# Expert tiles of 256, 192 and 128 slots in one form, and a routing step rearranged beside the last SwiGLU

## The chip, the cores and the metric

The kernel runs on one core of one Trainium2 chip. The core has a matrix engine (TensorE, "PE" in the profile, its weight loads "PEld"), a vector engine (VectorE, DVE), an activation engine (ScalarE, ACT), a general engine (GpSimd, POOL) and a queue engine (SyncE, SP) that issues most transfers. The metric is the time of one execution in device microseconds; the kernel before takes 730.28 us, the median of three runs (728.83 to 730.33). All times below are microseconds unless marked ns.

## The reference

The input x has 8 sequences of 256 tokens with 256 features, 2048 tokens in all. Four layers follow, each with a residual sum; all arithmetic is fp32.

```
x = x + L0(x)   # conditioned RMS norm, attention of 16 heads, conditioned RMS norm, SwiGLU of width 1024
x = x + L1(x)   # attention with a key mask, RMS norm of its output, modulation by the condition
x = x + L2(x)   # a fixed 4x4 rotation per feature (quaternions, with a gate)
x = x + L3(x)   # mixture of experts:
    gate = xn @ wg_W + wg_b + (genre_embed @ gg_W + gg_b)
    topk_w, topk_i = top_k(softmax(gate), 2)
    h1 = relu(x @ W1[e] + b1[e]); h2 = relu(h1 @ W2[e] + b2[e]); y = h2 @ W3[e] + b3[e]
    out = sum over a token's two experts of weight * y
```

L3 has 8 experts (256 to 512 to 512 to 256). With two experts per token there are 4096 pairs of token and expert, called slots here. Evaluated on these inputs, the reference's routing gives the experts 173, 190, 600, 732, 754, 773, 450 and 424 slots.

## The kernel before, in words

The tokens go through L0, L1 and L2 by sequence (b = 0 to 7), as a pipeline. The list `queue` fixes the order of attention steps (`block`, four per sequence and layer), and `run` puts pieces of other work between them: projections, SwiGLU pieces, normalisations. TensorE's instructions run in the order of the text throughout; up to the last attention, VectorE's and ScalarE's do too (`text_order`), so an instruction that waits holds up everything written after it on its engine. Most matmul results pass through three rotating PSUM banks (`bank`, pool `ps_m`): a fourth result waits until the first has been read.

`swiglu(b)` (lines 1082 to 1095) makes eight pieces of products, pg and ph in turn, each of four fp32 matmuls. pg is turned into sg by ScalarE and VectorE, ph is multiplied with it into hT, and then come four pieces of the output product pd.

Two sequences make a group (g = 0 to 3, 512 tokens). `rotate` (lines 1156 to 1167) applies L2 and writes the group's rows to the DRAM tables `tokens` and `out`; `route` (1179 to 1237) finds each token's two experts; `place_choices` (1244 to 1261) counts places with the matmul pk, and POOL scatters a record of token number and weight into the DRAM list `slots`, where each expert has a region of its own.

`table` turns the experts' counts into a list of tiles: which expert, and where its records begin. It is a chain of tiny VectorE instructions on one partition. The first table is made when three of four groups are routed: five tiles of 256 slots are sure to be full by then, whatever the last group holds. The second, after the last group, gives the rest: 12 whole tiles and, with `half_table`, two places for half tiles, for experts whose rest is 128 slots or fewer. Tiles beyond that would run in a conditional part after the main one.

`experts` runs a list of tiles as a pipeline on TensorE. Per tile: `records` reads the slot records (SP), `fetch` the expert's weights (SP, 2180 KB, three buffers in turn), `gather` the tokens' rows (POOL), `flip` transposes them, `hidden` makes h1 and h2 (weights stationary, 256 slots as columns, lines 1461 to 1471), `give` makes y with the slots stationary and adds the rows into `out` by indirect DMA (1489 to 1509). Within tile n the order is h1 of n, y of n-1, flip of n+1, h2 of n. A half tile is made in another form by `half` (1524 to 1555): its 128 slots are stationary and 512 weight columns move past them; each hidden layer is then transposed back by four transposes. Its steps are laid between those of a whole tile.

At the start of the kernel, `conditioned` flips the first sequence into one bank, VectorE scales both halves of it (line 912), and a few dummy matmuls (`keep_busy`, tile pw) fill TensorE meanwhile. Near the end of the pipeline, the loop step i = 6 has `late_=(4,)`: the follow-up of block 4, `after_second(4)` with its copies o<-py (line 1129), is held back until block 5 has been issued.

## Time and profile before

| what | value |
|---|---|
| median of three runs | 730.28 |
| profiled execution | 731.9 |
| its span, first to last instruction | 729.7 |
| TensorE busy | 710.9 (97%) |
| VectorE, ScalarE, POOL busy | 366.0, 258.7, 183.1 |
| expert tiles begin, last matmul ends | 452, 720 |
| granted TensorE clock, mean | 0.988 |

A group of instructions is shown as line, engine, operation, result and operands by the program's names, shapes and count. A busy time of matmuls counts each pass from issue to result, and passes overlap, so what one costs is read from the distance between starts. A wait is printed as who waited, for which instruction, how long in total, how often, and the longest. In a stretch's row come the busy times of PE, PEld, DVE, ACT and POOL, each with its count, then the granted clock, the share of DMA time and GB/s. In a timeline a row has start, duration, engine, line, operation and operands, and in square brackets the idle time before it with what ended it.

### The profile page before, as it was taken

Reading aid. Unit: us, or ns where it says so; the run is one execution under the profiler, and the core shown is the slowest. Engines: PE = TensorE matmul, PEld = TensorE weight load, DVE = VectorE, ACT = ScalarE, POOL = GpSimd, SP = SyncE. Lnnn points to the kernel's source line nnn. Section 1 sums busy time; section 2 is a strip of 40 time slices with the busy share of each in tenths; the row PEclk is TensorE's granted clock in tenths of the full one; section 3 lists DMA queues with packets and bytes.
Section 4 is the critical chain, followed back from the end, with each engine's and each line's share of the span. In section 5 each row is a group of like instructions: output and inputs, shape, how many; then the busy total and the mean of one; then the engine's idle time right before and its main releaser. Section 6 shows DMA issues by size and latency. Waiting matters only on the chain.

```text
span 729.7 us, 11080 instructions
## 1 busy us (share of the span) xinstructions
PE 710.9 (97%) x4242; PEld 539.5 (74%) x4242; DVE 366.0 (50%) x1129; ACT 258.7 (35%) x414; POOL 183.1 (25%) x219
## 2 busy tenths in 40 slices
PE   8999999999999999999999989999999999999994
PEld 7567777667666766766677856788888788788883
DVE  5557444575586764586854754777122222222221
ACT  2653335444454444454542315332121222221220
POOL 4312601000001311000500044126452424433113
PEclk9999999999999999999999989999999999999997
DMA  9400000000010000010000225464784586676512
GB/s 300 149 16 16 0 1 15 12 4 16 15 60 14 16 1 1 15 58 1 17 1 1 73 90 177 178 195 139 220 258 152 166 275 188 203 241 236 158 15 33
DMA packets 27005, 68.03 MB, mean 93 GB/s; under 512 B 8312, under 2 KB 21120, under 8 KB 24512
## 3 DMA queue, kind: packets, MB, share of 16 engines
q1 hardware_dynamic: 17904, 55.21, 22.0%
q0 software_dynamic: 8752, 11.85, 7.5%
q8 instruction: 35, 0.57, 0.4%
q14 instruction: 26, 0.21, 0.1%
q10 hardware_dynamic: 288, 0.18, 0.1%
HBM read 57.44 MB, written 9.79 MB: 92 GB/s over the span
## 4 chain that ended last, share of the span: by engine, by line
PE 89%; DVE 6%; ACT 1%; issue 1%; DMA 0%; POOL 0%; POOLq 0%; DVEq 0%; ACTq 0%
PE ph_a L1461 17%; PE s_a L976 9%; PE pg L1082 8%; PE o_a L989 8%; PE pd L1095 8%; PE ph L1082 8%; PE pe_a L1489 5%; PE ph_s L1461 5%; PE pq_a L920 4%; PE pk_a L920 4%; PE py L1012 2%; PE pv_a L950 2%; PE py L1128 2%; PE pe_s L1489 2%; PE pv_a L942 2%; PE ph_a_h L1534 1%
## 5 line engine op out<-in xcount | busy, mean ns | idle before, releaser
L978 ACT ACTIVATE pe_a<-s_a 128x2048 f32<-128x2048 f32 x64 | 120.1, 1877 | 116.9 <-PE s_a L976 116.7
L1461 PE MATMUL ph_a<-h_a,w_a 128*128 128x256 f32 x384 | 85.5, 379 | 0.0
L1461 PEld LDWEIGHTS ph_a<-h_a,w_a 128*128 128x128 f32 x384 | 72.1, 190 | 10.2 <-issue 1.0
L976 PE MATMUL s_a<-qz_a,kT_a 32*128 32x512 f32 x512 | 74.1, 647 | 0.7 <-ACT pe_a L978 0.2
L1471 DVE TENSOR_SCALAR h_a<-ph_a,w_a 128x256 f32<-128x256 f32 x48 | 23.2, 483 | 92.1 <-PE ph_a L1461 91.1
L1082 PE MATMUL pg<-xT_n,gate_wT 128*128 128x256 f32 x256 | 61.9, 385 | 0.0
L989 PE MATMUL o_a<-pe_a,va 128*32 128x256 f32 x1024 | 61.9, 382 | 0.0
L1082 PE MATMUL ph<-xT_n,hid_wT 128*128 128x256 f32 x256 | 61.5, 383 | 0.0
L1095 PE MATMUL pd<-out_wT,hT 128*128 128x256 f32 x256 | 61.1, 392 | 0.0
L989 PEld LDWEIGHTS o_a<-pe_a,va 128*32 128x32 f32 x1024 | 30.0, 109 | 39.9 <-issue 23.4
L1095 PEld LDWEIGHTS pd<-out_wT,hT 128*128 128x128 f32 x256 | 49.0, 195 | 13.6 <-issue 4.0
L1469 ACT ACTIVATE h_a<-ph_a,w_a 128x256 f32<-128x256 f32 x48 | 22.8, 475 | 97.8 <-DVE h_a L1471 97.8
L1082 PEld LDWEIGHTS ph<-xT_n,hid_wT 128*128 128x128 f32 x256 | 47.8, 190 | 13.0 <-DVE y L1054 3.0
L1082 PEld LDWEIGHTS pg<-xT_n,gate_wT 128*128 128x128 f32 x256 | 47.5, 190 | 12.7 <-issue 3.2
L1509 POOL DMA_INDIRECT out<-ye_a,trec_a x24 | 38.0, 1584 | 63.3 <-ACT ye_a L1507 53.4
L1055 POOL TENSOR_TENSOR xy<-y,x 128x512 f32<-128x512 f32 x8 | 10.2, 1271 | 142.1 <-DVE y L1054 87.2
L1461 PE MATMUL ph_a<-xt_a,w_a 128*128 128x256 f32 x192 | 43.7, 379 | 0.0
L998 DVE STREAM_TRANSPOSE tu_a<-o_a 128x512 f32<-128x512 f32 x32 | 22.8, 712 | 39.5 <-PE o_a L989 39.5
L1261 POOL DMA_INDIRECT slots<-rec,posi x32 | 31.8, 995 | 42.4 <-DVE r_mine L1251 32.9
L1489 PE MATMUL pe_a<-w_a,h_a 128*128 128x256 f32 x184 | 42.1, 379 | 0.0
L1461 PEld LDWEIGHTS ph_a<-xt_a,w_a 128*128 128x128 f32 x192 | 36.3, 190 | 4.9
L1489 PEld LDWEIGHTS pe_a<-w_a,h_a 128*128 128x128 f32 x184 | 34.7, 190 | 5.7 <-issue 1.0
(310 smaller groups left out, 1062.6 us busy)
## 6 DMA issues: line engine op xcount, KB each, us to landing
w_a<-in_experts SPq DMA_DIRECT2D x12, 2180.0 KB, 9.3
w_s<-in_experts SPq DMA_DIRECT2D x5, 2180.0 KB, 10.3
w_a_h<-in_experts SPq DMA_DIRECT2D x2, 2180.0 KB, 9.1
mod<-mod_rows SPq DMA_DIRECT2D x8, 256.0 KB, 3.3
tokens<-x SPq DMA_DIRECT2D x4, 512.0 KB, 3.2
out<-x SPq DMA_DIRECT2D x4, 512.0 KB, 4.2
x<-in_x SPq DMA_DIRECT2D x7, 256.0 KB, 2.8
gate_wT<-in_gate_wT SPq DMA_DIRECT2D x1, 1024.0 KB, 9.0
```

What stands on the lines that cost most here:

```text
L920: nc.tensor.matmul(pp[:, c, :], w[:, k, c * P : (c + 1) * P], xT[:, k, :], start=k == 0, stop=k == KC - 1)
L976: nc.tensor.matmul(sc[:, j], kT[r, c, kc * P : (kc + 1) * P], qz[r, c], start=True, stop=True)
L978: nc.scalar.activation(pe, sc, AF.Exp)
L989: nc.tensor.matmul(o[32 * i : 32 * i + 32, qd, :], va[:, kc, 8 * c + 4 * qd + i].rearrange("p a d -> p (a d)"), pe[:, 2 * qd + i // 2, i % ...
L998: nc.vector.transpose(turned.rearrange("p q j a d -> p (q j a d)"), o.rearrange("p q s -> p (q s)"))
L1082: nc.tensor.matmul(ps[:, j, :], w[:, k, o : o + P], yT[:, k, :], start=k == 0, stop=k == KC - 1)
L1095: nc.tensor.matmul(pd[:, t, :], hT[:, c, t * P : (t + 1) * P], out_w[:, c, :], start=c == 0, stop=c == HID // P - 1)
L1261: sc = nc.gpsimd.indirect_dma_start(out=slots, out_offset=bass.IndirectOffsetOnAxis(ap=posi[:, t : t + 1], axis=0), in_=rec[:, t, :], in_o ...
L1461: nc.tensor.matmul(ph[:, c - c0, :], w[:, o : o + P], src[:, k, :], start=k == 0, stop=k == n_in - 1)
L1471: nc.vector.tensor_scalar(h[:, c, :], ph[:, c - c0, :], bias, 0.0, ALU.add, ALU.max)
L1489: nc.tensor.matmul(pos[q][:, q, :], h2[:, k, q * P : (q + 1) * P], w[:, o : o + D], start=k == 0, stop=k == MC - 1,)
L1509: ad = nc.gpsimd.indirect_dma_start(out=out[0:reach, :], out_offset=bass.IndirectOffsetOnAxis(ap=rec[:, q, 0:1], axis=0), in_=y[:, q, :], ...
```

## The change

- Tiles have one form in three sizes: 256 slots (two column blocks of 128), 192 (two of 96) and 128 (one). All run weights-stationary through `hidden` and `give`, one after another in the order `ORDER`; `half` is gone. The rest is now 9 whole tiles, three of 192 and two of 128. `parts_table` lists both smaller kinds, by the count of full steps of 64 slots.
- One sure tile, the early one, is listed from the first two groups (`first_table`, now run in loop step 6 right after `place_choices(1)`); the other four by `second_table`, beside the first block of the last `run("bbb")`. The early tile's weights, record and rows are asked for when its pools open, before the last two sequences' work.
- In the last group of pieces before `place_choices(2)`, the steps of the rotation and routing of group 2 stand differently among the SwiGLU pieces: (0, 0, 1, 1, 2, 1, 2, 0) pieces ahead of the eight steps and two after them, instead of (0, 2, 1, 1, 2, 1, 1, 0) and one.
- The first sequence is flipped into two banks, and ScalarE scales the second half.
- Two memsets on POOL stand before four of its loads instead of after them.

```
-HALF = SL // 2
-NBIG = (2 * T + E * (HALF - 1)) // SL
-ALWAYS = 12
-HALVES = 2
-
-BESIDE = (3, 6)
+QUARTER = SL // 4
+SMALLER = ((2, 96), (1, 128))
+NBIG = (2 * T + E * (QUARTER - 1)) // SL
+ALWAYS = 9
+PARTS = (3, 2)
+
+ORDER = "ww1w0w1w0w0www"
...
     quats = small_in[:, 0 : B + 4 + 1]
+    for va in va_bufs["a0"]:
+        nc.gpsimd.memset(va, 1.0)
     wcT = load(nc.gpsimd, a["WcT"], [C, 2 * D], "WcT", pool=pool_b)
...
-    def conditioned(xs, b, j, name, eng=(nc.vector, nc.vector)):
-        pt = flipped(xs, name)
+    def conditioned(xs, b, j, name, eng=(nc.vector, nc.vector), apart=False):
+        if apart:
+
+            pts = [bank(f"pt_{name}_{k}", (P, S)) for k in range(KC)]
+            for k in range(KC):
+                for t in range(NQ):
+                    nc.tensor.transpose(pts[k][:, t * P : (t + 1) * P], xs[:, t, k * P : (k + 1) * P], ident)
...
+        nt = row(f"nt_{key}", [E])
+        nc.vector.tensor_tensor(nt, each[:, :, nh - 1], done[:, 0:E], ALU.subtract)
...
+        if op is ALU.is_ge:
+
+            now = row(f"now_{key}", [E])
+            nc.vector.tensor_tensor(now, end, nt, ALU.subtract)
+            nc.vector.tensor_scalar(now, now, -1.0, float(n_tiles), ALU.mult, ALU.add)
+            nc.vector.scalar_tensor_tensor(now, now, 0.0, nt, ALU.max, ALU.min)
+            nc.vector.tensor_tensor(done[:, 0:E], done[:, 0:E], now, ALU.add)
+        return end, each
+
+    def parts_table(each):
+
+        n = row("n_p", [2, E])
+        nc.vector.tensor_tensor(n[:, 0, :], each[:, :, 2], each[:, :, 3], ALU.subtract)
+        nc.vector.tensor_tensor(n[:, 1, :], each[:, :, 0], each[:, :, 2], ALU.subtract)
...
     def first_table():
-        nt, end, todos["sure"], _ = table("sure", (NG - 1) * NTG, SURE, ALU.is_ge)
...
+        table("early", (NG - 2) * NTG, EARLY, ALU.is_ge)
+        yield
+
+    def second_table():
+        table("sure", (NG - 1) * NTG, SURE - EARLY, ALU.is_ge)
         yield
...
+    def whole(key, n):
+
+        return f"{key}{n}", lambda what: todos[key][0:1, what, n : n + 1], NQ2, P
+
+    def smaller(size, n):
+        return f"p{size}_{n}", lambda what: todos["parts"][0:1, what, size, n : n + 1], *SMALLER[size]
+
+    def experts(items, pl, key, early=0, near_end=None):
...
         def hidden(n, src, n_in, off, boff, name):
-            w = st[n]["w"]
+            w, many = st[n]["w"], items[n][2] * items[n][3]
...
                         nc.tensor.matmul(
-                            ph[:, c - c0, :], w[:, o : o + P], src[:, k, :], start=k == 0, stop=k == n_in - 1
+                            ph[:, c - c0, 0:many], w[:, o : o + P], src[:, k, 0:many],
+                            start=k == 0, stop=k == n_in - 1,
                         )
...
-        placed = at_once(place_choices(i // 2 - 2)) if i in (4, 6) else once(compare_queries) if i == 2 else iter(())
+        placed = {
+            2: lambda: once(compare_queries), 4: lambda: at_once(place_choices(0)),
+            6: lambda: at_once(place_choices(1), first_table()),
+        }.get(i, lambda: iter(()))()
...
     pl = expert_pools(life_a, life_b2)
+    others_ = []
+    sure = experts(
+        [whole("early", n) for n in range(EARLY)] + [whole("sure", n) for n in range(SURE - EARLY)],
+        pl, "s", EARLY, near_end=(next(others_[0]) for _ in range(1)),
+    )
+    next(sure)
...
-    for n in (0, 2, 1, 1, 2, 1, 1, 0):
+    for n in (0, 0, 1, 1, 2, 1, 2, 0):
         for _ in range(n):
             next(pieces)
         next(rotated, None)
     do(rotated)
     next(pieces)
+    next(pieces)
     do(place_choices(NG - 2))
-    do(first_table())
-    others_ = []
-    near_end = (next(others_[0]) for _ in range(1))
-    sure = experts(0, SURE, todos["sure"], pl, "s", True, near_end=near_end)
-    next(sure)
-    run("bbb", pieces, 20.0)
+    run("bbb", pieces, 20.0, {0: [second_table(), sure]})
```

## The prediction

> **What bounds the kernel now.** First the page's busy line, then the busy time by stretch, then the waits of TensorE, then three timelines. All times are microseconds from the start of the profiled span.

> ```profile
> PE 710.9 (97%) x4242; PEld 539.5 (74%) x4242; DVE 366.0 (50%) x1129; ACT 258.7 (35%) x414; POOL 183.1 (25%) x219
> ...
> 421.00:425.00 4.00, 0.53 (x3) 0.30 (x2) 3.42 (x19) 0.00 (x0) 0.00 (x0) 1.00 0.00 0
> 425.00:432.00 7.00, 6.87 (x22) 4.58 (x22) 5.14 (x34) 1.88 (x1) 3.89 (x4) 0.52 0.02 3
> ...
> 533.00:717.00 184.00, 184.00 (x862) 157.48 (x861) 43.21 (x95) 40.30 (x87) 61.09 (x46) 1.00 0.60 181
> ...
> 8.90:12.20 3.30, 3.13 (x13) 2.98 (x14) 1.96 (x12) 1.20 (x5) 1.27 (x2) 0.50 1.08 344
> ```

> TensorE is the bound. In the stretch of the expert tiles (533 to 717) it is never idle, with VectorE and DMA far from full: what a tile costs there is what its matmuls cost. Column seven after the span is the granted clock: it is halved in 425 to 432 and in 8.9 to 12.2.

> ```profile
> PE pk L1244 <- DVE r_both L1232: 3.8, 2, 3.5
> PE pw L1787 <- POOL ident masks.py:199: 1.5, 1, 1.5
> PE pt_n L884 <- DVE aff L632: 1.4, 1, 1.4
> ```

> The longest wait of TensorE is the routing of group 2: pk stands 3.5 behind VectorE's r_both. The timeline there, TensorE alone:

> ```profile
> 419.31 1.89 PE L1095 MATMUL pd<-out_wT,hT 128*128 128x256 f32 x8
> 424.67 0.38 PE L1244 MATMUL pk<-r_both,before 128*128 128x32 f32 x2 [3.48 <-DVE r_both L1232]
> 425.18 0.59 PE L1245 MATMUL pk<-seen,ones 128*128 128x32 f32 x2
> 425.59 0.57 PE L1298 MATMUL pcount_sure<-seen,ones 128*128 128x8 f32 x2
> 426.09 2.09 PE L976 MATMUL s_a<-qz_a,kT_a 32*128 32x512 f32 x8
> ```

> After the gap the s_a group takes 2.09, where it takes 1.14 elsewhere. The idle 3.48 is followed by 6.83 at half clock, so this place loses 3.5 and then 3.4. Now the price of a pass. An fp32 matmul is two passes in the trace, so an x8 group is four matmuls:

> ```profile
> 576.35 1.88 PE L1534 MATMUL ph_a_h<-w_a_h,xt_a_h 128*128 128x512 f32 x4
> 578.07 1.89 PE L1489 MATMUL pe_a<-w_a,h_a 128*128 128x256 f32 x8
> 579.80 0.60 PE L1542 MATMUL pth_a_h<-ident,hs_h_a_h 128*128 128x128 f32 x4
> 580.23 1.89 PE L1489 MATMUL pe_a<-w_a,h_a 128*128 128x256 f32 x8
> ...
> L754 PE MATMUL pgconst<-small_in,cond_b x16: 252/252/273, 35.3 to 37.0; 64*128 64x8 f32 x16
> ...
> L843 PE MATMUL phall<-scaled,wo1n x8: 219/275/275, 78.3 to 79.0; 128*128 128x64 f32 x8
> ```

> Passes overlap, so the start-to-start time counts. 512 columns: 1.72/4 = 430 ns. 256: (579.80 - 578.07)/8 = 216. A 128-column transpose: 0.43/4 = 109. The price goes with the columns (0.84 ns each), down to a floor where a fresh weight rides with each pass: first to last start of pgconst (8 columns) give 1.7/15 = 113 ns, of phall (64 columns, 128x128 weights) 0.7/7 = 100. I take 112. The last timeline is the routing of group 1 in step 6 of the loop:

> ```profile
> 350.57 0.17 DVE L1259 COPY rec<-r_top 128x4 f32<-128x4 f32 x1
> 350.64 0.77 DVE L1129 COPY o<-py 128x264 f32<-128x264 f32 x2
> 350.71 0.60 PE L884 MATMUL pt_n<-ident,xs_n 128*128 128x128 f32 x4
> 351.14 0.64 PE L884 MATMUL pt_x<-ident,x 128*128 128x128 f32 x4
> ```

> **The change, part by part.** The sum is made against the profiled execution: 731.9 in all, span 729.7. The median of the runs shown is 1.6 lower.

> *Tile sizes.* The reference's routing of these inputs gives experts 173, 190, 600, 732, 754, 773, 450 and 424 slots: by the new classes 14 whole tiles (5 sure, 9 later), three of up to 192 and two of up to 128. So all places are filled and the path for leftovers is not taken. Before it is 17 whole and two halves; fetches stay at 19. A 192 tile has 24 hidden matmuls, 48 passes, of 192 columns. No row has that width; between 128 (109) and 256 (216) the line gives 162. Gain 48 x 54 ns = 2.6, three times 7.8. Its eight output matmuls keep 256 columns, and its flips are taken as equal. An old half is 2 x 109 + 12 x 430 + 8 x 109 + 8 x 216 ns = 7.97. The new 128 tile is 2 x 109 + 48 x 112 + 8 x 216 = 7.32, so two of them gain 1.3. Together -9.1. The bad end takes the 190 ns that a weight load shows as busy time for the pace of a pass: the 192 tiles then gain 3.7 and the 128 tiles lose 6.2, +2.5 in all. I take -9.1, because phall and the transposes with the same kind of weight run at 112 and below.

> The stretch 533 to 717 was granted clock 1.00 with two halves and their 128-column transposes in it, so I charge thin passes no clock. [...] Padded, this part would be 0 and the sum +2.7.

> Cover: a weight of 2180 KB lands in 9.3; the shortest time from the release of its buffer to its use is the end of a 128 tile and a whole one, some 16.5. SP waits for buffers today, not TensorE for SP. If that cover went, each short tile would pay up to 3. The evacuations (0.48 and 0.47) shrink with the columns and lie beside at least 1.8 of the next tile's first matmuls. The longer parts table adds some 1.5 to VectorE near 500 to 505; its numbers are fetched at 511.8, so nothing. POOL issues fewer gathers and adds per short tile (1.0 and 1.6 each), no bound.

> *Routing beside the last swiglu.* Nine swiglu pieces precede pk as before. But the rotation's first two steps now stand ahead of them on VectorE, and the route's two last steps pass ahead of the last product. Followed on VectorE in text order with the durations of before (times of before in brackets): the squares end at 411.6 (414.6), the chain up to the exponential at 416.9 (419.9), r_both at 422.3 (424.5). TensorE would finish pd at 421.1 and start pk at 422.45, not 424.67: -2.2. Ends: 0, if a swiglu bank waits instead, and -3.5, the whole gap. What is late next is hT of the last piece, at 423.8, needed only after the scores.

> Clock: 3.4 were lost here. Left are 1.35 idle and a few tenths between the two pk. The nearest row is the start: idle of 1.4 before pt_n, then half clock from 8.8 to 12.2, which would lose 1.7 again. Gaps of 0.4 and 0.7 near 398 cost no clock. Between 1.7 and 3.4 gained I take 2.6.

> [...]

> *The early table in step 6.* This adds a wait. first_table now follows place_choices(1) at block 4, in text order on VectorE, ahead of the copies o<-py (L1129), which step 6 holds back to block 5. Of the table of before, 22 instructions took 427.22 to 431.4; the new one has 27 on a single row, about 4.8 at 0.18 each. So o starts at 355.45, its first copy (0.43) ends at 355.9, and pt_x, which rotates through three banks and needs that copy's bank (count now takes one more), starts at 355.95 and not 351.14: +4.8 of TensorE time, with scores, values and projections queued behind. VectorE's queue behind moves by as much, so the stall isn't won back. Ends: 0, if a free bank lies between, and 6. Clock: 4.8 idle lies nearest the 3.48 gap, which lost 3.4; part of the half clock falls into the stall itself, and only the rest of 6.8 counts, so 1.4 to 3.4: +2.5.

> *The second table* runs after x of the last swiglu, in VectorE's idle time (4.2 before 435.6, 2.2 before 438.5); 5 of work delays tu_a by 2.9 and qz by 0.3. +0.2, ends 0 and 2.9. One more count matmul is 0.2, and the count that no longer stands before s_a returns that.

> *Moved issues.* The early tile's weight, record and two gathers go from 431 to 448 up to about 363. SP's next there is mod at 401.84; POOL idles 23.78 before 397.58. Hidden; with that gone, the mod row has 30 to spare. The later records still wait for the scatters, as at 441.

> *Start.* Two banks let ScalarE take half of xT: it ends 0.45 sooner. But the dummy matmuls pw occupy TensorE until 11.23, when pk_a starts anyway: 0, ends -0.5 and 0.2. The two memsets (1.87) now precede four POOL loads, first used at 16.7.

> Sum: -9.1 - 2.2 - 2.6 + 4.8 + 2.5 + 0.2 = -6.4, so 725.5 for a profiled execution and **723.9** against the median.

> **The rivals.**
> 1. *The table is hidden* (a bank is free, or the o copies come first): the 7.3 fall away, 716.6. For it: VectorE is half idle over the span. Against: it is busy 5.58 of 6 from 351 to 357, and its order is fixed there.
> 2. *The routing gap stays*, since the swiglu's banks wait behind the rotation instead: 4.8 less gain, 728.7. For it: three banks only; against: the product of piece 1 is written 2 before its bank is wanted.
> 3. *Slower: the weight load sets the pace of thin passes.* Place: the five short tiles; price 190 ns per pass, +11.6 against my sum, 735.5. It decides from 169 ns: (169 - 112) x 96 + (169 - 162) x 144 ns = 6.5, my 6.4. For it: 190 is the busy time of L1461's load; against: phall's pace.
> 4. *A count differs by a token or two* (450 has two slots above its class): then the leftover path runs, at least a fetch (9.3) and a tile (14) with its adds, above 750.

> **How the numbers follow.** Chances: forecast 0.52 (720.5 to 727 alone), rival 1 0.22, rival 2 0.14, rival 3 0.08, rival 4 0.04. From 715.5 to 729.5 lie the forecast, nearly all of rival 1 and most of rival 2, about 0.82. About 0.2%, 1.5, is what a measurement can tell: faster takes the forecast, rival 1 and half of rival 2 (0.80), the same is most of its rest (0.07), slower rivals 3 and 4 and a little (0.13).

> **What the profile after would show.** ph passes of 192 columns starting every 162 ns and of 128 every 112; pk's wait at about 1.3; a wait of pt_x for o of about 4.8 near 351, with the clock halved behind it; the clock after the routing at 1.00 or halved for one window. What would make me wrong is above all the stall in step 6, the largest term that no row shows, and the clock behind both gaps.

## The result, and the profile after

The changed kernel takes 722.6 us in the median (721.75 to 724.7, five runs) beside 730.28 of the kernel before (728.65 to 731.68, five runs). The ratio is 0.9907, with a 95% interval of 0.9882 to 0.9932. The profiled execution of the changed kernel took 722.57, its span 720.8; the sum above was made against a profiled execution of 731.9 and a span of 729.7, and the spans differ by 8.9.

The page's busy line of the changed kernel:

```profile
PE 700.9 (97%) x4300; PEld 537.7 (75%) x4300; DVE 370.7 (51%) x1166; ACT 256.4 (36%) x411; POOL 181.6 (25%) x219
```

TensorE is still the bound, 10.0 less busy than before. What it waited for, in us in total, how often, and the longest wait:

```profile
PE pt_x L888 <- DVE o L1143: 4.0, 1, 4.0
PE pk L1258 <- DVE r_both L1246: 1.7, 2, 1.3
...
PE pt_n L914 <- DVE aff L636: 0.9, 1, 0.9
...
PE s_a L988 <- DVE qz_a L946: 0.4, 1, 0.4
```

The wait of pk for r_both has shrunk from 3.5 to 1.3, and a wait of pt_x for the copy o, which the list before did not have, has come in with 4.0. The busy time by stretch (start:end, length, then PE, PEld, DVE, ACT and POOL with counts, the granted clock, DMA share, GB/s) says where the clock fell:

```profile
8.48:11.89 3.41, 3.40 (x13) 3.18 (x14) 1.61 (x9) 1.47 (x5) 1.47 (x2) 0.50 1.06 303
...
353.23:360.05 6.82, 4.97 (x32) 2.22 (x36) 6.20 (x31) 3.37 (x6) 5.29 (x6) 0.50 0.04 4
...
424.00:431.00 7.00, 5.54 (x30) 3.90 (x29) 5.86 (x30) 0.85 (x2) 0.23 (x1) 1.00 0.01 2
534.00:709.50 175.50, 175.50 (x921) 157.03 (x921) 42.00 (x95) 37.77 (x84) 59.87 (x46) 1.00 0.61 188
```

The clock is halved at the start, as before, and from 353.23 to 360.05, behind the new wait, and no longer behind the routing. In the expert tiles TensorE is never idle and the clock is full, as before. Three timelines (start, duration, engine, line, operation, operands, idle before it) show the three places. First step 6 of the loop:

```profile
350.20 0.15 DVE L1319 TENSOR_SCALAR count_early<-pcount_early 1x8 f32<-1x8 f32 x1
...
354.52 0.15 DVE L1368 TENSOR_TENSOR done<-done,now_early 1x8 f32<-1x8 f32 x1
354.61 0.75 DVE L1143 COPY o<-py 128x264 f32<-128x264 f32 x2
355.08 1.11 PE L888 MATMUL pt_x<-ident,x 128*128 128x128 f32 x4 [4.01 <-DVE o L1143]
```

VectorE works through the early table from 350.20 to 354.67, then makes the copies o, and pt_x starts behind the first of them. Then the routing of group 2:

```profile
425.19 1.89 PE L1109 MATMUL pd<-out_wT,hT 128*128 128x256 f32 x8
428.41 0.38 PE L1258 MATMUL pk<-r_both,before 128*128 128x32 f32 x2 [1.33 <-DVE r_both L1246]
...
429.26 1.14 PE L988 MATMUL s_a<-qz_a,kT_a 32*128 32x512 f32 x8
```

The scores behind it take 1.14, not 2.09. Last, the tiles:

```profile
559.09 1.95 PE L1489 MATMUL ph_a_p<-xt_a_p,w_a_p 128*128 128x128 f32 x16
560.87 3.62 PE L1519 MATMUL pe_a_rest<-w_a_rest,h_a_rest 128*128 128x256 f32 x16
...
580.79 2.76 PE L1489 MATMUL ph_a_p<-xt_a_p,w_a_p 128*128 128x192 f32 x16
583.39 3.62 PE L1519 MATMUL pe_a_rest<-w_a_rest,h_a_rest 128*128 128x256 f32 x16
```

Sixteen passes of 128 columns take 1.78 from start to next start, 111 ns each; sixteen of 192 columns take 2.60, 162.5 ns each.

Cutting both traces at four matmuls that both have gives the ledger. The marks are the first pk_a of the group that starts near 302, the first pk_a of the group near 399 to 405, the first h1 matmul of the first later tile (533 to 534), and the last start of an output matmul.

| stretch | before | after | difference | predicted |
|---|---|---|---|---|
| start to pk_a near 302 | 302.80 | 302.35 | -0.45 | 0 |
| to pk_a near 400, with step 6 | 96.09 | 102.42 | +6.33 | +7.3 |
| to the first later tile, with the routing | 134.49 | 129.48 | -5.01 | -4.6 |
| the later tiles | 186.38 | 177.13 | -9.25 | -9.1 |
| rest | 9.94 | 9.38 | -0.56 | 0 |
| span | 729.7 | 720.8 | -8.9 | -6.4 |

### The profile page after: what moved, and what is told of

Same layout as the page of the kernel before. It is cut to its first block, busy times and chain, and to the rows that moved or that the text cites. A ratio compares the mean times of both kernels' runs of the same rounds, so it can differ in the third digit from the quotient of the medians.

```text
span 720.8 us, 11237 instructions
## 1 busy us (share of the span) xinstructions
PE 700.9 (97%) x4300; PEld 537.7 (75%) x4300; DVE 370.7 (51%) x1166; ACT 256.4 (36%) x411; POOL 181.6 (25%) x219
## 4 chain that ended last, share of the span: by engine, by line
PE 89%; DVE 6%; ACT 1%; issue 1%; DMA 0%; POOL 0%; POOLq 0%; DVEq 0%; ACTq 0%
PE ph_a_rest L1489 13%; PE s_a L988 9%; PE pg L1096 8%; PE o_a L1001 8%; PE ph L1096 8%; PE pd L1109 7%; PE ph_a_p L1489 5%; PE pe_a_rest L1519 4%; PE ph_s_sure L1489 4%; PE pq_a L932 4%; PE pk_a L932 4%; PE py L1024 2%; PE pe_a_p L1519 2%; PE pv_a L962 2%; PE py L1142 2%; PE pv_a L954 2%
## 5 line engine op out<-in xcount | busy, mean ns | idle before, releaser
L1489 PE MATMUL ph_a_rest<-h_a_rest,w_a_rest 128*128 128x256 f32 x288 | 63.7, 379 | 0.0
L1489 PEld LDWEIGHTS ph_a_rest<-h_a_rest,w_a_rest 128*128 128x128 f32 x288 | 54.1, 190 | 7.0
L1109 PE MATMUL pd<-out_wT,hT 128*128 128x256 f32 x256 | 59.2, 383 | 0.0
L1500 DVE TENSOR_SCALAR h_a_rest<-ph_a_rest,w_a_rest 128x256 f32<-128x256 f32 x36 | 17.4, 484 | 73.5 <-PE ph_a_rest L1489 72.5
L1498 ACT ACTIVATE h_a_rest<-ph_a_rest,w_a_rest 128x256 f32<-128x256 f32 x36 | 17.1, 474 | 77.3 <-DVE h_a_rest L1500 77.3
L1533 POOL DMA_INDIRECT out<-ye_a_rest,trec_a_rest x18 | 28.5, 1581 | 39.1 <-ACT ye_a_rest L1531 30.0
L1102 DVE SCALAR_TENSOR_TENSOR sg<-th,pg 128x512 f32<-128x512 f32 x32 | 21.9, 685 | 28.2 <-ACT th L1100 28.2
L988 PEld LDWEIGHTS s_a<-qz_a,kT_a 32*128 32x128 f32 x512 | 20.4, 184 | 18.9 <-issue 12.5
L1100 ACT ACTIVATE th<-pg 128x512 f32<-128x512 f32 x32 | 19.0, 593 | 40.8 <-PE pg L1096 40.7
L1489 PE MATMUL ph_a_rest<-xt_a_rest,w_a_rest 128*128 128x256 f32 x144 | 32.6, 379 | 0.0
```

What stands on the lines that cost most here:

```text
L988: nc.tensor.matmul(sc[:, j], kT[r, c, kc * P : (kc + 1) * P], qz[r, c], start=True, stop=True)
L1102: nc.vector.scalar_tensor_tensor(sg, th, 1.0, pg, ALU.add, ALU.mult)
L1109: nc.tensor.matmul(pd[:, t, :], hT[:, c, t * P : (t + 1) * P], out_w[:, c, :], start=c == 0, stop=c == HID // P - 1)
L1489: nc.tensor.matmul(ph[:, c - c0, 0:many], w[:, o : o + P], src[:, k, 0:many], start=k == 0, stop=k == n_in - 1,)
L1533: ad = nc.gpsimd.indirect_dma_start(out=out[0 : reach(n), :], out_offset=bass.IndirectOffsetOnAxis(ap=rec[0:p, q, 0:1], axis=0), in_=y[0:p ...
```

## The experiments

Every edit is made to the changed kernel. The median of the kernel before, on the same chip at the same time, was 731.25 us for experiments 1 to 4, 730.71 for 5 and 7 to 9, and 731.07 for 6 and 10; the changed kernel, run again with these last, took 723.56 (seven runs). Medians of one kernel move by some 1 us from one set of runs to the next, so small effects are read from distances inside a trace, with the marks of the table above.

**1. The table of the sure tile is moved out of step 6.**

```
-            6: lambda: at_once(place_choices(1), first_table()),
+            6: lambda: at_once(place_choices(1)),
...
-    next(sure)
     n2 = in_parts(B - 1, "n2")
-    run("bbbvn", pieces, 3.8, {0: [n2]}, soon=2, ...)
+    run("bbbvn", pieces, 3.8, {0: [n2], 2: [first_table(), sure]}, soon=2, ...)
```

With the table goes `next(sure)`, the first step of the early tile's pass (its transfers), so both leave step 6.

> The table of the sure tile and the first step of its expert pass leave step 6 of the loop and stand behind the second block of the stretch that follows the loop. Theory (the table's VectorE operations are queued ahead of the o copies, so pt_x of sequence 5 waits, and the clock is halved behind that wait): the 4.0 us wait at pt_x goes, the two halved windows behind it go (2.2 us), the count matmul moves to a place where it costs 0.25 either way: 722.6 - 6.2 = 716.4, and the granted clock is 1.00 from 350 to 362. Rival (the wait only moves to where the table now stands, with a new idle of TensorE of 3 us or more there): 720 to 724.

Measured: 717.16 (715.54 to 718.82, five runs), ratio to the kernel before 0.982 (0.9801 to 0.9838). In its timeline around the place:

```profile
348.49 0.17 DVE L1273 COPY rec<-r_top 128x4 f32<-128x4 f32 x1
348.56 0.77 DVE L1143 COPY o<-py 128x264 f32<-128x264 f32 x2
348.62 0.60 PE L888 MATMUL pt_n<-ident,xs_n 128*128 128x128 f32 x4
349.06 0.64 PE L888 MATMUL pt_x<-ident,x 128*128 128x128 f32 x4
```

and in its stretches:

```profile
344.00:352.00 8.00, 8.00 (x67) 5.26 (x69) 6.06 (x23) 4.54 (x7) 4.22 (x4) 1.00 0.01 2
352.00:420.00 68.00, 66.15 (x398) 49.45 (x390) 48.40 (x148) 25.29 (x41) 10.55 (x13) 1.00 0.19 61
```

The copies o follow the last rec at once, pt_x follows pt_n without idle, and the clock is full throughout. From the mark near 302 to the next it takes 96.93, against 102.42 in the changed kernel and 96.09 before: at the new place the table costs 0.84, of which 0.47 is a new wait of py for oT_a. So 5.5 of the 6.33 came from that place, and the timeline says how: by the order on VectorE. The theory holds; the rival's wait of 3 us did not come.

**2. The old order of the pieces beside the rotation.**

```
-    for n in (0, 0, 1, 1, 2, 1, 2, 0):
+    for n in (0, 2, 1, 1, 2, 1, 1, 0):
...
     do(rotated)
     next(pieces)
-    next(pieces)
     do(place_choices(NG - 2))
```

> The pieces beside the rotation of sequence 5 are put back into the order (0,2,1,1,2,1,1,0), with one piece left for the place ahead of the last choices. Theory (the rearranged pieces are what shortened the routing wait, and the clock drop behind it followed from the wait): pk waits about 3.5 us again instead of 1.33, +2.1, and the clock behind it is halved again, +2 to +3.4: 726.5 to 728. Rival (the wait alone is back, the clock does not follow): 724.7. Second rival (the wait went for another reason, the earlier tables): 722.6.

Measured: 726.21 (723.82 to 728.3, six runs), ratio 0.9929 (0.9908 to 0.995). Timeline of TensorE, then the stretches behind it:

```profile
427.04 1.89 PE L1109 MATMUL pd<-out_wT,hT 128*128 128x256 f32 x8
432.41 0.38 PE L1258 MATMUL pk<-r_both,before 128*128 128x32 f32 x2 [3.48 <-DVE r_both L1246]
```

```profile
430.53:433.94 3.41, 1.40 (x12) 0.91 (x12) 2.67 (x15) 0.00 (x0) 0.00 (x0) 1.00 0.00 0
433.94:437.35 3.41, 3.41 (x14) 2.19 (x7) 0.82 (x7) 1.88 (x1) 2.18 (x3) 0.50 0.01 1
```

The gap is 3.48 again, to the hundredth what it was before the change, and the clock falls behind it, here for one stretch of 3.41 where the kernel before had 6.83. From the mark near 400 to the first later tile it takes 133.26, against 129.48: 2.15 of gap and 1.6 of clock. The order of the pieces is what closed the gap. The median is 0.3 below the range expected; in this profile the clock fell for one stretch and not two.

**3. Whole columns in the middle size.**

```
-SMALLER = ((2, 96), (1, 128))
+SMALLER = ((2, 128), (1, 128))
```

> The two tiles of 192 slots are done at 256 columns, all else the same (two tiles of 256 columns more, the added columns blank). Theory (time of a column goes by its columns, 216 ns for 256 and 162.5 for 192, the weight load is not what paces): 48 passes a tile and matrix set as counted before, +2.6 us a tile for each of three such tiles: 722.6 + 7.8 = 730.4. Rival (the passes of 192 are paced by something else than their columns, so that the gain came from fewer tiles or from the order): within 1 us of 722.6.

Measured: 730.75 (728.3 to 732.38, ten runs), ratio 0.9995 (0.9982 to 1.0007). In the expectation, the count of tiles is to be read as: the same tiles, three of them with 256 columns where they had 192. Timeline:

```profile
580.88 3.62 PE L1489 MATMUL ph_a_p<-xt_a_p,w_a_p 128*128 128x256 f32 x16
584.33 3.62 PE L1519 MATMUL pe_a_rest<-w_a_rest,h_a_rest 128*128 128x256 f32 x16
```

Sixteen passes take 3.45 and not 2.60. The stretch of the later tiles takes 185.05 against 177.13, +7.92 for three tiles, where 7.8 was expected; everything ahead of it agrees with the changed kernel's trace within 0.02. With this one edit the whole change is worth nothing against the kernel before: the 64 columns that three tiles leave out are as much as all that is left of it.

**4. Unused matmuls in the gap of step 6.**

```
+        if b == 5:
+            pw = ps_o.tile([P, 2, S], F32, tag="o", name="pw_5")
+            for _ in range(17):
+                nc.tensor.matmul(pw[:, 0, 0:P], ident, ident, start=True, stop=True)
         pt = flipped(x2, f"x2_{b}")
```

> 17 matmuls of 128 columns that nobody reads stand ahead of pt_x of sequence 5, where TensorE idles 4.0 us. Theory (the clock is halved because of the idle before it): the granted clock stays at 1.00 from 350 to 362, pt_x comes at the same time, and what follows it is 2.2 us earlier: 720.4. Rival (the clock falls for another cause, or the added matmuls only push pt_x back): 722.6 to 724.

Measured: 722.22 (720.72 to 722.59, four runs), ratio 0.988 (0.986 to 0.99). Timeline, then the stretch:

```profile
352.31 3.96 PE L1123 MATMUL pw<-ident 128*128 128x128 f32 x34
356.49 0.65 PE L888 MATMUL pt_x<-ident,x 128*128 128x128 f32 x4 [0.22 <-DVE o L1147]
```

```profile
353.23:360.05 6.82, 6.60 (x72) 4.52 (x70) 5.99 (x34) 3.26 (x6) 5.26 (x6) 1.00 0.04 4
```

pt_x comes where it came without them (356.49; in experiment 2, whose profile has nearly the same start, 356.58), and the clock is full from 353.23 to 360.05, where experiment 2 has 6.83 of half clock from 355.43. Mark to mark step 6 takes 100.38, against 102.42 in the changed kernel and 102.76 in experiment 2: the half clock behind the stall costs 2.0 to 2.4, and it is the idle that brings it. It is the trace that shows this and not the total: the median misses the 720.4 expected by 1.8 and lies just below the rival's 722.6; in the profile the start alone is 1.4 longer: the first mark is reached at 303.76 and not 302.35 (see experiment 10 and the last section).

**5. A tenth piece ahead of the last choices, with the moved table.**

```
     next(pieces)
     next(pieces)
+    next(pieces)
     do(place_choices(NG - 2))
```

> The moved table of the first experiment, and a third piece of the last swiglu issued ahead of the last choices, where pk still waits 1.33 us for r_both. Theory (the wait is only a lack of TensorE work at that place; a piece is about 1.9 us of work that is to be done in any case): pk no longer waits, nothing is added: the moved table's 717.2 less 1.3 = 715.9. Rival (the piece's VectorE work, or the copies that it calls for, stand ahead of r_both or of the next block's first operations and the wait moves there): 717 to 718.5.

Measured: 716.87 (715.26 to 720.17, four runs), ratio 0.9813 (0.9788 to 0.9838). Timeline:

```profile
420.97 0.19 DVE L1246 TENSOR_TENSOR r_both<-r_sel,r_sel 128x32 f32<-128x32 f32 x1
421.19 0.77 DVE L1251 TENSOR_TENSOR seen<-seen,r_both 128x8 f32<-128x8 f32 x4
421.88 0.68 DVE L1104 TENSOR_TENSOR hT<-sg,ph 128x512 f32<-128x512 f32 x1
...
422.62 1.13 PE L1109 MATMUL pd<-out_wT,hT 128*128 128x256 f32 x4 [1.78 <-DVE hT L1104]
423.59 0.30 PE L1258 MATMUL pk<-r_both,before 128*128 128x32 f32 x2
```

pk no longer waits; half of the tenth piece does, for an hT that stands behind r_both and the four seen on VectorE. The rival's mechanism is right: the wait moves, and from the mark near 400 to the first later tile it takes 129.17, against 129.47 with the moved table alone. The median is 0.1 below the rival's 717 and 1.0 above the theory's 715.9.

**6. The pieces still later, with the moved table.** Two orders with three pieces left for the end, none added: (0,0,1,1,1,1,2,0), and

```
-    for n in (0, 0, 1, 1, 2, 1, 2, 0):
+    for n in (0, 0, 0, 1, 2, 1, 2, 0):
...
     next(pieces)
     next(pieces)
+    next(pieces)
     do(place_choices(NG - 2))
```

> The moved table, and the pieces beside the rotation in the order (0,0,1,1,1,1,2,0) with three in place of two behind it: one of the nine is done later, none is added. In the moved table's trace pk waits 1.34 us for r_both, which ends a chain of VectorE instructions (r_sm at 417.83 to r_both at 420.95) that stands behind the swiglu's sg and hT. Theory (a piece done later leaves its sg and hT behind the chain, and its matmuls in the gap): pk waits 0 to 0.6, 717.2 - 0.7 to - 1.3 = 716.2. Rival (as with the tenth piece, the matmuls of the last piece wait for an hT that now stands behind the chain): pk or pd wait 1.3 to 2.0, 717 to 718.

> The same, with the first of the pieces held back in place of a later one: (0,0,0,1,2,1,2,0) and three behind. Theory (only how many pieces are left behind the chain counts): the same as with the order before it, 716.2. Rival (the rotation's first steps then have no TensorE work beside them, a new wait of 1 us or more shows ahead of the first piece): 717 to 719.

Measured: 717.03 (715.35 to 718.28) and 716.7 (714.63 to 717.88), five runs each, ratios 0.9797 (0.9775 to 0.982) and 0.9796 (0.9774 to 0.9818). The second in its timeline:

```profile
420.06 1.89 PE L1109 MATMUL pd<-out_wT,hT 128*128 128x256 f32 x8
422.79 0.41 PE L1258 MATMUL pk<-r_both,before 128*128 128x32 f32 x2 [0.84 <-DVE sg L1102]
```

Both leave 0.84 of 1.34, where at most 0.6 was expected of the first; it also opens a new wait of 0.44 ahead of a pg. Mark to mark it is 129.35 and 128.94, so 0.1 and 0.5 are gained over the moved table, less than medians can tell. Both gains are smaller than expected: a delayed piece also puts its sg into the chain that pk waits for.

**7. Twice the unused matmuls at the start.**

```
-        keep_busy(4, "pw1")
+        keep_busy(8, "pw1")
```

> Eight unused matmuls in place of four ahead of the first flips. The profiles so far show three starts: half clock from 8.5 to 11.9 us behind an idle of 0.95 (the changed kernel), no half clock behind an idle of 1.30 (the moved table), and half clock from the first matmul to about 10.5 us with no idle (two others). Theory A (the idle before pt_n brings the half clock): with 0.5 us of idle or none left the clock is full from 5 us on, 721 to 721.6. Theory B (the clock is set in stretches of 3.41 us whose marks lie differently in every execution, and what is idle matters less than where the marks fall): the three starts still occur, and where the clock is at half the four added matmuls push pt_n back by 0.9: 722.3 to 723.5.

Measured: 723.51 (721.42 to 724.56, four runs), ratio 0.9894 (0.9875 to 0.9914). Stretches:

```profile
8.50:11.90 3.40, 3.40 (x22) 3.14 (x22) 1.98 (x12) 1.47 (x5) 1.46 (x2) 1.00 1.07 338
36.09:39.50 3.41, 3.41 (x10) 2.70 (x9) 0.00 (x0) 0.58 (x1) 0.00 (x0) 0.50 0.00 0
```

No idle is left ahead of pt_n and the clock stays full there, but it is halved later, at 36.09, in a place without idle. The first pk_a near 302 starts at 302.40, against 302.35: nothing gained. This speaks for theory B in the main: the half stretch was not avoided, it fell elsewhere. The added matmuls are not needed for that: with four of them the half stretch lies at 36.63 in the second version of experiment 6 and at 36.65 in experiment 9. A start at half clock, with the flips pushed back, was not in this profile.

**8. The memsets of va put back**, and **9. the first flips in one bank**, one run each (722.22 and 723.26), for single instructions and not for the total.

```
     quats = small_in[:, 0 : B + 4 + 1]
-    for va in va_bufs["a0"]:
-        nc.gpsimd.memset(va, 1.0)
...
         do(first_norm(1))
+        for va in va_bufs["a0"]:
+            nc.gpsimd.memset(va, 1.0)
```

> The memsets of va go back behind the first norms on GpSimd's queue. One look at single instructions, not at the total. Theory (a VectorE instruction that runs beside GpSimd's memset is held up): the instructions that took 1.40 (rq_v_n, before the change) and 1.35 us (xs_n, after it) are long exactly where a memset lies beside them, so rq_v_n takes 1.4 us again and xs_n 0.35. Rival (the long instruction belongs to its own operands, or to the loads that land then): xs_n stays at 1.35, rq_v_n at 0.17.

```
-            s.pop("xs1"), b, 0, f"n1_{b}", (nc.vector, nc.vector if b else nc.scalar), apart=b == 0
+            s.pop("xs1"), b, 0, f"n1_{b}"
```

> The first flips go back into one bank, and both halves of xT_n are copied by VectorE. One look at the time between the first flip and the first pk_a, not at the total. Theory (the copies were not what the first pk_a waited for, since unused matmuls filled that time already): 2.2 us from the first flip to the first pk_a as with two banks at half clock, within 0.2; no gain of the two banks. Rival (the copies set it): 0.3 to 0.5 us longer.

One row of the kernel before, then VectorE, GpSimd and the first flip in the changed kernel:

```profile
5.02 1.40 DVE L612 TENSOR_SCALAR rq_v_n<-ss_n 128x2 f32<-128x2 f32 x1
...
4.80 0.17 DVE L616 TENSOR_SCALAR rq_v_n<-ss_n 128x2 f32<-128x2 f32 x1
...
6.99 1.35 DVE L902 TENSOR_SCALAR xs_n<-x,rq_y_n 128x256 f32<-128x256 f32 x1
6.99 0.54 POOL L730 MEMSET blank<- 128x520 int32 x1
...
7.65 0.54 POOL L734 MEMSET zero<- 128x512 f32 x1
...
8.49 1.09 PE L914 MATMUL pt_n<-ident,xs_n 128*128 128x128 f32 x4 [0.95 <-DVE aff L636]
```

and with the memsets of va put back:

```profile
4.38 1.87 POOL L1778 MEMSET va<- 128x1024 f32 x2
4.70 1.72 DVE L614 TENSOR_SCALAR rq_v_n<-ss_n 128x2 f32<-128x2 f32 x1
...
8.56 0.35 DVE L900 TENSOR_SCALAR xs_n<-x,rq_y_n 128x256 f32<-128x256 f32 x1
...
9.06 0.66 PE L912 MATMUL pt_n<-ident,xs_n 128*128 128x128 f32 x2 [1.39 <-DVE aff L634]
```

The same two instructions change places: the one that lies beside a memset is long, the other short, as expected. pt_n starts at 9.06 again, as before the change (9.07), and at 8.49 with the memsets ahead. That is the step at the start that gains: 0.57, from a memset's place on GpSimd. At the mark near 302 the two profiles, both with a half stretch at 8.5, stand at 302.68 and 302.35, so 0.33 of it is left there. With one bank, first flip to first pk_a is 1.27 at full clock (8.48 to 9.75); with two banks, at full clock, 1.14 in the profile of experiment 7 (8.48 to 9.62). At half clock one bank took 2.16 in the kernel before (9.07 to 11.23) and two banks 2.16 in the changed one (8.49 to 10.65). So the two banks are worth 0.13 at most.

**10. The changed kernel once more.**

> The changed kernel once more, beside the two versions with the moved table. Theory (the clock is set in stretches of 3.41 us whose marks lie differently in each execution, so that the same instructions lose 0 to 3.4 us near the start and 1.7 to 3.4 behind the 4.0 us stall): a profile whose half-clock stretches differ from those of the first (8.48 to 11.89, 353.23 to 360.05), at a median of 722 to 723.5. Rival (the stretches belong to the kernel): the same two stretches within 0.1 us.

Measured: 723.56 (720.39 to 724.5, seven runs), ratio 0.9895 (0.9877 to 0.9913). Stretches of its profile:

```profile
8.50:11.90 3.40, 3.40 (x21) 3.14 (x22) 1.97 (x12) 1.47 (x5) 1.47 (x2) 1.00 1.05 294
351.01:354.43 3.42, 0.97 (x8) 0.73 (x12) 3.11 (x18) 0.96 (x5) 2.81 (x3) 1.00 0.03 2
354.43:357.84 3.41, 3.41 (x28) 0.99 (x24) 2.99 (x15) 2.40 (x3) 2.49 (x4) 0.50 0.07 7
```

Same instructions, same wait of 4.01 at pt_x, but no half clock at the start and one half stretch behind the wait in place of two. Mark to mark the start takes 300.73 and not 302.35, step 6 101.73 and not 102.42; the two stretches behind them agree within 0.02, and the end is 0.14 longer. The theory fits: two executions of one kernel differ by 2.2 of span, and the difference lies in the two stretches in which the clock fell differently.

**11. GpSimd's other memsets ahead of its loads**, with the order (0,0,0,1,2,1,2,0) and the moved table.

```
     for va in va_bufs["a0"]:
         nc.gpsimd.memset(va, 1.0)
+    blank = work.tile([P, TABLE // P, 4], I32, tag="oS", name="blank")
+    nc.gpsimd.memset(blank, 0)
+    zero = pool_b.tile([P, SL // P, D], F32, tag="xs", bufs=3, name="zero")
+    nc.gpsimd.memset(zero, 0.0)
     wcT = load(nc.gpsimd, a["WcT"], [C, 2 * D], "WcT", pool=pool_b)
```

> The version with the moved table and the first piece held back, and GpSimd's memsets of blank and zero ahead of its four loads, behind those of va. Theory (VectorE's xs_n takes 1.35 us in place of 0.35 because these two memsets lie beside it at 6.99 to 8.19): xs_n takes 0.35 to 0.4, the first flip comes at 7.5 to 8.1 and no longer at 8.49, limited by the unused matmuls that end at 7.2 to 8.1: 716.7 less 0.4 to 1.0. Rivals (another VectorE instruction is caught by the memsets at their new place: the flip stays at 8.5 or comes later; or the four loads, now 1.1 later, are waited for: later than 8.5).

Measured: these runs were on another chip, on which the kernel before took 753.45 (750.58 to 757.1, eleven runs); the version took 731.53 (729.97 to 734.16, six runs), ratio 0.9712 (0.9681 to 0.9744). The totals can't be set beside the others. The start can:

```profile
6.89 0.39 DVE L902 TENSOR_SCALAR xs_n<-x,rq_y_n 128x256 f32<-128x256 f32 x1
...
7.62 0.60 PE L914 MATMUL pt_n<-ident,xs_n 128*128 128x128 f32 x4
```

xs_n takes 0.39 and the first flip comes at 7.62, 0.87 sooner, as expected. On that chip TensorE also waited 2.6 and 3.6 at two pv_a (256.6 and 364.4), where it doesn't in the other profiles; why was not settled, so whether the 0.87 reaches the end on the first chip stays open, and the version was not run there.

## Why the prediction was right, and where it was off

The direction, the place and the size are right; the time is 1.3 below the forecast. By its steps:

- *Tile sizes*, -9.1: -9.25 measured. The 192-column pass, for which no row stood in the trace of before, costs 162.5 ns by the line between 109 and 216 that gave 162; the 128-column pass costs 111 to 112. The third experiment gives the three middle tiles +7.92 when their columns are put back. Rival 3 (190 ns a pass) is refuted. The stretch kept clock 1.00, so padding the short tiles to 256 columns would have given back 7.9 on the middle tiles alone, with no clock to gain. Rival 4, a leftover path, did not come about. The 128 tiles were not changed by themselves: 9.25 less 7.92 leaves 1.33 for the two, where the sum has 1.3. The prediction's price of padding is too low: by its own pass times the two 128 tiles, padded to 256 columns, cost 5.0 more each (48 x 104 ns), so this part would be near +8.7 (-9.1 + 7.8 + 10.0) and not 0; no run padded them. Two slips in its working carry nothing: 0.43/4 is 108 ns and not 109, and an old half adds up to 7.98.
- *Routing*, -2.2: the gap went from 3.48 to 1.33, -2.15, and the second experiment brings exactly that gap back by the order alone. Rival 2 falls.
- *Clock behind the routing*, -2.6 between 1.7 and 3.4: no half clock behind 1.33 of idle. The row of the start (1.4 idle, then half clock), to which the lower end was tied, is no guide to this place; in the profiled pair the stretch gained 5.01 in all, which with 2.15 of gap leaves about 2.9 for clock and counts together, so the 2.6 was on the low side. What it is worth depends on the execution compared with: the same gap of 3.48 brought 6.83 of half clock in the kernel before and 3.41 in the second experiment.
- *Early table in step 6*, +4.8 and +2.5: the mechanism is right in all its steps (the order on VectorE, the held-back copies, the bank, the clock behind it), and the first experiment shows it by taking the table away. The term was mis-sized: with the start's -0.45 taken out, pt_x came 4.39 later than before (355.08 + 0.45 - 351.14) and not 4.8, 4.01 of it idle, since the 27 instructions follow each other at 0.16 (4.41 from 350.20 to 354.61) and not 0.18. The clock was worth 2.0 to 2.4, by experiment 4, and not 2.5. Rival 1 falls.
- *Second table*, +0.2: a wait of 0.4 of s_a for qz_a.
- *Start*, 0: this step failed. It looked at the banks and at the unused matmuls, and gave the moved memsets no price but their loads. pt_n came 0.57 sooner, because a memset of GpSimd no longer lies beside rq_v_n (0.17 and not 1.40); the banks gave nothing at half clock, as said. The bounds (-0.5 to 0.2), drawn from ScalarE's half of xT, held what reached the next mark, -0.45, by luck and not by their reason; 0.33 of it is the memset by experiment 8, the rest was not traced.
- *Moved issues*: the early weights were asked for at 386.79 and not "up to about 363": by the profile SyncE waited 26.9 ahead of that issue for ScalarE's xs_n, which reads here as memory that was still in use. No wait of TensorE for them is in the list, so the 0 stands.

What is left is the end behind the last output matmul, -0.56, which no step covers and whose cause is open (it takes 9.38 to 9.72 in the versions run here), and that the sum was made on one profiled execution. The forecast of -6.4 stands against -8.9 in the two profiled executions and -7.7 in the medians; part of that spread is the clock's marks (two executions of the changed kernel lie 2.2 of span apart in experiment 10), which the prediction treated as fixed costs of the kernel.

The best version here is the changed kernel with the table moved behind the second block after the loop and the first piece held back: 716.7 beside 723.56 of the changed kernel in the same set of runs, and 731.07 before. Nearly all of that is the moved table.

## What to carry to other kernels

When work is moved into a part of the program where an engine runs in text order, ask which later instruction of that engine frees a buffer that TensorE needs: a table of 27 tiny instructions ahead of two copies cost 6.3 us where it stood and 0.8 two blocks later. The price of a column in a full matmul stretch could be read from neighbouring widths (162 expected of 192 columns, 162.5 measured), and it was won in full where TensorE never waits (-9.1 expected, -9.25 measured). Before a wait on the bounding engine is closed by more work, follow what that work itself waits for: a tenth piece and later pieces only moved the wait to their own hT (1.78) and sg (0.84).

## What the runs showed of the hardware

**Two VectorE instructions are held up beside a memset of GpSimd**, until about the memset's end: rq_v_n takes 1.40 and 1.72 in place of 0.17, xs_n 1.35 in place of 0.35 to 0.39, switched on and off by moving the memsets (experiment 8; experiment 11, whose other edits come later in the program). rq_v_n ends at 6.42 where the memset of va ends at 6.25, in the kernel before and in experiment 8, and xs_n at 8.34 where that of zero ends at 8.19, in the changed kernel. The runs show the delay and not its cause. Not every instruction is held: in the kernel before, the reduction ss_n lay beside the memset of va, and rq_p_n beside that of zero, and they kept their 0.42 and 0.16.
